# Queries of the first attention, pairs 2 to 7: seven half-size products for eight, with five weight sums read from DRAM

## The chip, the cores and the metric

The kernel runs on one core of a Trainium2 chip. The core has a matrix engine (TensorE, "PE" in the profile, with its weight loads as "PEld"), VectorE ("DVE"), ScalarE ("ACT"), GpSimd ("POOL") and SyncE ("SP"), whose queue does nothing here but start DMAs. Each engine works through its own instructions in order, and they wait for one another through semaphores. Matmuls write to PSUM, which has eight banks of 128 x 512 float32. [...]

The metric is the time of one execution in microseconds on the device. Before the change it is 1499.09 us (median of three runs, 1498.25 to 1500.35).

## The reference, cut to what matters

A token tensor `x` of 16 batches x 128 tokens x 512 passes through two layers, each an attention over a context of 16 x 128 x 128 and a feed-forward part with experts. All arithmetic is float32. What the change touches is the first attention:

```python
q_hk = (hidden_q @ Wq.T).reshape(b, s, H, K)            # H = 16 heads
q_big = jnp.einsum('bshk,hkq->bshq', q_hk, w_kc_q)
q_r = jnp.einsum('bshq,hqr->bhsr', q_big, W_qr)         # R = 64 per head
k_r = jnp.einsum('bld,hdr->bhlr', kv_rope, W_kr)
scores = jnp.einsum('bhsr,bhlr->bhsl', q_r, k_r)
attn = jax.nn.softmax(scores, axis=-1)
ctx_c = jnp.einsum('bhsl,bld->bhsd', attn, kv_rope)
ctx_lat = jnp.einsum('bhsd,hkd->bhsk', ctx_c, w_kc_kv)
out = ctx_lat.reshape(b, s, H * K) @ Wo.T
...
x = x + jnp.tanh(g_xattn[0]) * _L0_xattn_ref(_layernorm(x, axis=-1), ctx_512, ...)
```

## The kernel before, in words

The three weight matrices of the queries are multiplied together once, in the fold at the start: `fq` is a 512 x 1024 matrix (16 heads x 64), held as 128 partitions x 4 chunks x 1024. A query is then one product: 512 normalised features by 1024 columns.

Batches are taken in pairs `v` of two, 256 tokens. The queries of pairs 0 and 1 are made within the fold (`query` with 512 tokens). Those of pairs 2 to 7 are made in `keys_and_queries(v)`: for each of four banks, two head pairs by four chunks, eight matmuls with a 128x128 block of `fq` as weights and 256 tokens moving, then an eviction by VectorE or ScalarE in turn (`evacuate`), then two key matmuls into another bank and their eviction. A float32 matmul is two instructions in the profile (and two weight loads).

Pair 2's queries are made between the first softmaxes: `carry(0)`, two steps of `keys_and_queries(2)`, `score(2)`, `carry(1)`, the other two steps. From then on an outer loop goes over u = 1 to 8 with v = u - 1. One step, in program order:

- loads of two later x tiles; `gather` (context by weights) of the even batch of pair v, `score(2u)`, `turn(u + 1)` (transposes of the normalised tokens of a later pair into `xnT`), `combine_next`;
- the projections of pair v (`project`, itself seven products for eight) with the softmax of batch 2u between them (`soften` on ScalarE and GpSimd, `block` on VectorE), then `carry(2u)`;
- `combine_next`, `score(2u + 1)`, the remaining projections with that batch's softmax, then `carry(2u + 1)`;
- stores of pair v for later (`xk`), `combine_next`, at odd u the context for a later group (`load_kv`), and last `keys_and_queries(u + 1)`, for u = 2 to 6.

`carry(b)` sends 16 small DMAs (128-byte pieces) that finish the transposition of the softmax. `combine_next` prepares weights of the feed-forward part: it writes a prepared block to DRAM (`w1_kept`, `w2_kept`), loads another (`quarters`) and has GpSimd make its sums. All these DMAs go through `send`, on SP's queue.

The order on an engine is not left to the compiler in this stage: `matmul`, `transpose` and `send`, and VectorE work passed to `pin`, are held in program order from `score(0)` on. SP waits in that order for what a DMA needs, and everything behind it waits too. PSUM banks: four of tag `mm` (`mm_tile`), two `tr`, two `acc`. Scores use `mm`; queries of this loop `tr`, keys `acc`.

In the lines of the profile, L169 is every ordered matmul and L174 every ordered transpose (both helpers); L179 is `send`; L85 and L87 are the two branches of `evacuate`; L546 is a matmul of `fold_second`, L534 a transpose of the fold; L639 and L640 are GpSimd sums of `fold_outward`; L703 and L709 belong to `soften` and `block`.

Of the kernel before, what the change touches and what calls it, by code (L numbers as in the profile page):

```python
# [9 lines left out]
F32 = mybir.dt.float32  # L10
AF = mybir.ActivationFunctionType
ALU = mybir.AluOpType
# [3 lines left out]
P = 128  # L16
NB = 16
# [5 lines left out]
H = 16  # L23
# [19 lines left out]
def kernel(  # L43
# [22 lines left out]
    def tr_tile(name):  # L66
        return ps_tr.tile([P, 512], F32, tag="tr", name=name)
# [7 lines left out]
    def pin(ins):  # L75
        if pinned[0]:
            tc.keep_in_program_order(ins)
# [3 lines left out]
    def evacuate(dst, src):  # L81

        flip[0] ^= 1
        if flip[0]:
            pin(nc.vector.tensor_copy(dst, src))  # L85
        else:
            nc.scalar.copy(dst, src)  # L87
# [290 lines left out]
    with tc.tile_pool(name="a0", bufs=2) as ap, tc.tile_pool(name="a0s", bufs=3) as sp:  # L378
# [34 lines left out]
        def query(dst, p, xnT):  # L413
            for c in range(ND):
                matmul(
                    dst, fq[:, c, ts(p, P)], xnT[:, c, :],
                    start=(c == 0), stop=(c == ND - 1),
                )

        def homes(what, v):  # L420
            twos = [
                ap.tile([P, 2, 2 * P], F32, tag=f"{what}{j}", name=f"{what}_{v}_{j}", bufs=1)
                for j in range(NPAIR // 2)
            ]
            return [t[:, i, :] for t in twos for i in range(2)], twos
# [23 lines left out]
                xns[v].append(xn)  # L449

        def turn(v, which=(0, 1)):
            g, h = divmod(v, 2)
            if h == 0 and which[0] == 0:
                turned[g] = lnp.tile([P, ND, GT], F32, tag="xnT", name=f"xnT_a0_{g}", bufs=1)
            for i in which:
                xn = xns[v][i]
                tr = (acc_tile if v == 2 else tr_tile)(f"xtr_a0_{v}_{i}")
                for c in range(ND):
                    transpose(tr[:, ts(c, P)], xn[:, ts(c, P)], ident)
                dst = turned[g][:, :, ts(2 * h + i, P)]  # L460
                if v == 2:
                    pin(nc.vector.tensor_copy(dst, tr.rearrange("p (c t) -> p c t", t=P)))
                else:
                    evacuate(dst, tr.rearrange("p (c t) -> p c t", t=P))

# [199 lines left out]
        def score(b):  # L667


            v, i = divmod(b, 2)  # L670
            tiles = [mm_tile(f"s_ps{b}_{t}") for t in range(4)]
            for p in range(NPAIR):
                for j in range(2):
                    rows = slice(j * R, (j + 1) * R)
                    matmul(
                        tiles[p // 4 * 2 + j][:, ts(p % 4, P)],
                        q_r[v][p][rows, ts(i, P)], k_r[v][p][rows, ts(i, P)],
                        start=True, stop=True,
                    )
            ebs[b] = rp.tile([P, NK, H, BK], F32, tag="eb", name=f"eb_{b}")  # L680
            eTs[b] = rp.tile([P, NK, H, BK], F32, tag="eT", name=f"eT_{b}")
            soft[b] = []
            for t in range(4):
                nmx = sp.tile([P, 4], F32, tag="nmx", name=f"nmx_a0_{b}_{t}", bufs=4)
                pin(nc.vector.tensor_reduce(  # L685
                    nmx, tiles[t].rearrange("p (i l) -> p i l", l=P), AX.X, ALU.max,
                    negate=True,
                ))
                soft[b].append((tiles[t], nmx))
# [18 lines left out]
        def block(b, t):  # L708
            pin(nc.vector.transpose(  # L709
                ebs[b][:, :, 4 * t : 4 * t + 4, :].rearrange("p k n i -> p n k i"),  # L710
                soft[b][t].rearrange("p n (k i) -> p n k i", k=NK),
            ))
# [43 lines left out]
        def project(v, n):  # L756
# [17 lines left out]
            for i, cols in targets:  # L774
# [2 lines left out]
                    dst, y_ps, gate_x[0], dst, ALU.mult, ALU.add  # L777
                ))

        def keys_and_queries(v):  # L780
            g, h = divmod(v, 2)
            half = slice(2 * h * P, (2 * h + 2) * P)
            (k_r[v], k_two), (q_r[v], q_two) = homes("k", v), homes("q", v)
            for j in range(NPAIR // 2):
                q_ps = tr_tile(f"q_ps{v}_{j}")
                for i in range(2):
                    query(q_ps[:, ts(i, 2 * P)], 2 * j + i, turned[g][:, :, half])
                evacuate(q_two[j], q_ps.rearrange("p (i t) -> p i t", i=2))
                k_ps = acc_tile(f"k_ps{v}_{j}")
                for i in range(2):  # L790
                    key(k_ps[:, ts(i, 2 * P)], 2 * j + i, roped[g][1][:, half])
                evacuate(k_two[j], k_ps.rearrange("p (i t) -> p i t", i=2))
                yield j


# [61 lines left out]
        ups = {}  # L857

        xk = [wd.tile([P, D], F32, name=f"xk_{n}") for n in range(KEPT)]
        ordered[0] = pinned[0] = True  # L860


# [6 lines left out]
        for p in range(7):  # L869
            fold_next(p)  # L870

            if p in (3, 5):
                turn(2, (p // 2 - 1,))
            if p % 2 == 0:
                soften(0, p // 2)
                if p:
                    block(0, p // 2 - 1)
        score(1)
        fold_next(7)
        block(0, 3)  # L880
# [889 lines left out]
```

## Time and profile before

| | |
|---|---|
| median of three runs | 1499.09 us |
| profiled execution, its own time | 1500.14 us |
| its span in the profile | 1498.3 us |
| TensorE busy | 1477.4 us (99%), 6752 instructions |
| weight loads busy | 997.9 us (67%) |
| VectorE, ScalarE, GpSimd busy | 832.9, 436.9, 466.5 us |
| DMA moved | 163.50 MB, mean 109 GB/s |
| queries of pairs 2 to 7 (128x256) | 384 instructions, 86.9 us busy |

The profile is of one execution. In the rows of groups and of the timeline, `out<-in` are the program's tile names without numbers, then the shape, then a count. Matmuls are pipelined: the length of one is its way through the array, and the distance of two starts is what it costs when they follow one another. "PEclk" is the granted clock of TensorE, 9 for full in the slices and 1.00 in the windows. A row with "SPq" is the time in which SP issues the DMA, not that of the transfer.

### The profile page before, as it was taken

How to read it: one execution, taken by the hardware profiler on the slowest of the kernel's cores; microseconds unless marked ns; L12 is line 12 of the kernel's file. 1: busy time of each engine (PE TensorE's matmuls, PEld its weight loads, DVE VectorE, ACT ScalarE, POOL GpSimd, SP SyncE). 2: the span in 40 equal slices, each digit the busy share in tenths (PEclk: the TensorE clock that was granted, in tenths of full speed). 3: DMA queues.
4: the chain of work that ended last, by engine and by line, in shares of the span. 5: the costliest groups of instructions: out<-in, count | busy, mean ns of one | idle time of the engine just before them, and what ended most of it. 6: DMA issues, size and time to landing. Idle time of an engine off the chain costs nothing. (4 is left out here: it accounts for less than half of the span.)

```text
span 1498.3 us, 19508 instructions
## 1 busy us (share of the span) xinstructions
PE 1477.4 (99%) x6752; PEld 997.9 (67%) x6752; DVE 832.9 (56%) x1722; ACT 436.9 (29%) x1432; POOL 466.5 (31%) x500
## 2 busy tenths in 40 slices
PE   7999999999999999999999999999999999999999
PEld 5567778778877666876678666876668444444444
DVE  2274644654656555655564656455556776757422
ACT  1262432432441122012210321022203565545310
POOL 1153533623422233204320442124414333324200
PEclk9999999999999999999999999999999999999999
DMA  7533645344244822452246222721242342323212
GB/s 265 144 94 94 188 140 153 111 119 125 64 81 139 249 74 74 122 151 74 74 113 159 74 74 72 197 90 63 80 136 71 76 127 71 84 61 90 64 29 99
DMA packets 142274, 163.50 MB, mean 109 GB/s; under 512 B 54096, under 2 KB 102224, under 8 KB 140000
## 3 DMA queue, kind: packets, MB, share of 16 engines
q1 hardware_dynamic: 139024, 157.13, 36.5%
q0 software_dynamic: 2016, 4.13, 1.1%
q8 instruction: 54, 0.88, 0.3%
q10 hardware_dynamic: 1136, 0.99, 0.2%
q14 instruction: 44, 0.36, 0.1%
HBM read 106.35 MB, written 18.09 MB: 83 GB/s over the span
## 5 line engine op out<-in xcount | busy, mean ns | idle before, releaser
L1130 POOL TENSOR_TENSOR near<-base,a 128x512 f32<-128x512 f32 x32 | 42.6, 1332 | 345.0 <-ACT base L1127 233.5
L201 POOL TENSOR_TENSOR e<-e,rden_a 128x512 f32<-128x512 f32 x64 | 66.6, 1040 | 164.5 <-DVE rden_a L199 141.8
L169 PE MATMUL q_ps<-xnT_a,fq 128*128 128x256 f32 (+1 forms) x448 | 115.8, 410 | 0.0
L1127 ACT ACTIVATE a<-a 128x512 f32<-128x512 f32 x64 | 40.3, 630 | 256.8 <-DVE a L1126 256.8
L169 PE MATMUL l_ps<-t,b_sb 128*128 128x512 f32 x256 | 115.1, 592 | 0.0
L696 ACT ACTIVATE e<-s_ps,nmx_a 128x128 f32<-128x128 f32 x256 | 90.2, 386 | 78.0 <-DVE nmx_a L685 40.4
L194 ACT ACTIVATE e<-e,nmx_a 128x128 f32<-128x128 f32 x256 | 98.8, 387 | 34.7 <-DVE nmx_a L189 34.7
L1126 DVE TENSOR_TENSOR a<-l_ps,base 128x512 f32<-128x512 f32 x64 | 44.0, 688 | 108.0 <-PE l_ps L169 107.9
L169 PEld LDWEIGHTS q_ps<-xnT_a,fq 128*128 128x128 f32 x448 | 84.8, 190 | 24.5 <-issue 12.5
L703 POOL TENSOR_TENSOR e<-e,rden_a 128x512 f32<-128x512 f32 x64 | 66.0, 1039 | 100.7 <-DVE rden_a L701 100.7
L169 PEld LDWEIGHTS l_ps<-t,b_sb 128*128 128x128 f32 x256 | 48.6, 190 | 59.5 <-issue 57.6
L169 PE MATMUL fy_ps<-ring,far 128*128 128x256 f32 x384 | 87.2, 380 | 0.0
L169 PE MATMUL y_ps<-fo_raw,c 128*128 128x256 f32 x384 | 85.8, 380 | 0.9 <-DVE c L85 0.9
L776 DVE SCALAR_TENSOR_TENSOR x<-y_ps,gates,x 128x256 f32<-128x256 f32 x112 | 48.7, 477 | 67.0 <-PE y_ps L169 66.9
L1192 DVE SCALAR_TENSOR_TENSOR x<-fy_ps,gw,x 128x256 f32<-128x256 f32 x112 | 46.5, 475 | 69.3 <-PE fy_ps L169 69.3
L169 PEld LDWEIGHTS fy_ps<-ring,far 128*128 128x128 f32 x384 | 72.6, 190 | 13.6 <-issue 4.0
L169 PEld LDWEIGHTS y_ps<-fo_raw,c 128*128 128x128 f32 x384 | 72.3, 190 | 10.7 <-ACT c L87 1.0
L1344 DVE STREAM_TRANSPOSE eb<-e 128x512 f32<-128x512 f32 x64 | 45.5, 712 | 42.0 <-POOL e L201 37.4
L169 PE MATMUL ht_ps<-T,ring 128*128 128x256 f32 x256 | 65.7, 379 | 0.0
L169 PE MATMUL t_ps<-a,a_sb 128*128 128x512 f32 x128 | 65.4, 592 | 0.0
L169 PE MATMUL t_ps<-base,a_sb 128*128 128x512 f32 x128 | 65.4, 592 | 0.0
L169 PE MATMUL y_ps<-fo_sums,c 128*128 128x256 f32 x256 | 60.4, 385 | 2.1 <-ACT c L87 0.8
(257 smaller groups left out, 2956.3 us busy)
## 6 DMA issues: line engine op xcount, KB each, us to landing
ring<-w SPq DMA_DIRECT2D x32, 896.0 KB, 4.5
eT<-eb SPq DMA_DIRECT2D x312, 64.0 KB, 2.0
ring<-w SPq DMA_DIRECT2D x16, 1024.0 KB, 5.3
ring<-in_f_w SPq DMA_DIRECT2D x12, 1024.0 KB, 6.1
wq<-in_wq SPq DMA_DIRECT2D x8, 512.0 KB, 6.1
x<-in_x SPq DMA_DIRECT2D x16, 256.0 KB, 4.6
quarters<-in_f_w SPq DMA_DIRECT2D x32, 128.0 KB, 2.5
w<-sums SPq DMA_DIRECT2D x8, 512.0 KB, 3.6
```

Of the source, the lines that this page charges most:

```text
L169: ins = nc.tensor.matmul(*args, **kw)
L194: nc.scalar.activation(dst[:, ts(i, P)], src[:, ts(i, P)], AF.Exp, bias=nmx[:, i : i + 1], accum_out=den[:, i : i + 1],)
L201: nc.gpsimd.tensor_tensor(d3, d3, rden.unsqueeze(2).to_broadcast([P, 4, P]), ALU.mult)
L696: nc.scalar.activation(e[:, ts(i, P)], s_ps[:, ts(i, P)], AF.Exp, bias=nmx[:, i : i + 1], accum_out=den[:, i : i + 1],)
L703: nc.gpsimd.tensor_tensor(e3, e3, rden.unsqueeze(2).to_broadcast([P, 4, P]), ALU.mult)
L776: pin(nc.vector.scalar_tensor_tensor(dst, y_ps, gate_x[0], dst, ALU.mult, ALU.add))
L1126: nc.vector.tensor_tensor(a, l_ps, base, ALU.add)
L1127: nc.scalar.activation(a, a, AF.Gelu_apprx_tanh)
L1130: nc.gpsimd.tensor_tensor(mix, base, second, ALU.add)
L1192: nc.vector.scalar_tensor_tensor(dst, y_ps[:, ts(i, half)], q.first[:, t : t + 1], dst, ALU.mult, ALU.add,)
L1344: nc.vector.transpose(by_blocks(ebs[b])[:, :, 4 * j : 4 * j + 4, :].rearrange("p k n i -> p n k i"), e.rearrange("p (n k i) -> p n k i", n ...
```

## The change

The product of a pair, 256 tokens x 512 features x 1024 columns, is cut into halves in all three directions: features (two chunks each), columns (heads 0 to 7 and 8 to 15, `near_q` and `far_q`), tokens (the two batches). Of the eight products of halves, seven are made, from sums of halves, after Winograd's form of Strassen's method: each product is four column blocks by two chunks of matmuls with 128 tokens moving. The parts:

- `query_sums()`, before `score(0)`: four sums or differences of quarters of `fq` (each 128 x 1024), three on GpSimd and one on VectorE; five of the seven weights are written to DRAM in ten DMAs, four on SP's queue and six on GpSimd's. The near columns of `fq` stay in place as two weights; the far columns become two places of 512 KB for streamed weights.
- `fetch()`: two sends of 256 KB that bring the next streamed weight into the place just used. Two fetches are made before `score(1)`; after that one follows each product with a streamed weight. Over a pair the products are made in the order 4, 0, 5, 1, 3, 2, 6 and the streamed ones among them are 4, 5, 3, 2, 6.
- `query_product(v, n, ...)`: eight matmuls into one bank (`tr` for pair 2, `mm` for the others), the fetch, and the additions into the result: ScalarE copies for products 4, 0 and 3, VectorE additions from PSUM for products 0, 5, 1, 2 and 6, two GpSimd additions after product 3. `u_2` holds a partial sum, in the tag of the normalised tokens.
- `keys_and_queries`: two products ahead of the first and of the second group of keys, product 3 ahead of the third, product 2 ahead of the fourth, product 6 after it.
- `turn`: the transposed tokens are kept per pair instead of per group of four batches, and four sums of them are made beside, two on VectorE and two on GpSimd.

```diff
+            if what == "q":
+                whole = ap.tile([P, NPAIR, 2, P], F32, tag="q", name=f"q_{v}", bufs=1)
+                return [whole[:, p].rearrange("p i t -> p (i t)") for p in range(NPAIR)], whole
...
         def turn(v, which=(0, 1)):
-            g, h = divmod(v, 2)
-            if h == 0 and which[0] == 0:
-                turned[g] = lnp.tile([P, ND, GT], F32, tag="xnT", name=f"xnT_a0_{g}", bufs=1)
+            if which[0] == 0:
+                turned[v] = lnp.tile([P, 2, ND, 2 * P], F32, tag="xnT", name=f"xnT_a0_{v}", bufs=1)
...
-                dst = turned[g][:, :, ts(2 * h + i, P)]
+                dst = turned[v][:, 0, :, ts(i, P)]
...
+            if which[-1] == 1:
+                b11, b12, b21, b22 = [
+                    turned[v][:, 0, 2 * k : 2 * k + 2, ts(i, P)]
+                    for k in range(2) for i in range(2)
+                ]
+                t_1, t_2, t_3, t_4 = [
+                    turned[v][:, 1, n].rearrange("p (c t) -> p c t", t=P) for n in range(4)
+                ]
+                pin(nc.vector.tensor_tensor(t_1, b12, b11, ALU.subtract))
+                pin(nc.vector.tensor_tensor(t_2, b22, t_1, ALU.subtract))
+                nc.gpsimd.tensor_tensor(t_3, b22, b12, ALU.subtract)
+                nc.gpsimd.tensor_tensor(t_4, b21, t_2, ALU.subtract)
+                turned[v] = [b11, b21, t_4, t_1, t_2, t_3, b22]
...
+        streamed = (4, 5, 3, 2, 6)
+        fq_kept = {
+            (n, h): wd.tile([P, 2, 2 * P], F32, name=f"fq_{n}_{h}")
+            for n in streamed for h in range(2)
+        }
+        near_q, far_q = slice(0, H * R // 2), slice(H * R // 2, H * R)
+
+        def query_sums():
+            a11, a12 = fq[:, :2, near_q], fq[:, 2:, near_q]
+            a21, a22 = fq[:, :2, far_q], fq[:, 2:, far_q]
+            two = rp.tile([P, 2, 2, H * R // 2], F32, tag="eT", name="fq_sums")
+            s_1, s_2 = two[:, 0], two[:, 1]
+
+            def keep(n, src):
+                for h in range(2):
+                    begin = nc.sync if n in (2, 5) else nc.gpsimd
+                    begin.dma_start(out=fq_kept[n, h], in_=src[:, :, ts(h, 2 * P)])
+
+            keep(2, a22)
+            nc.gpsimd.tensor_tensor(s_1, a21, a22, ALU.add)
+            nc.vector.tensor_tensor(a21, a11, a21, ALU.subtract)
+            keep(5, a21)
+            nc.gpsimd.tensor_tensor(s_2, s_1, a11, ALU.subtract)
+            keep(3, s_1)
+            keep(4, s_2)
+            nc.gpsimd.tensor_tensor(a22, a12, s_2, ALU.subtract)
+            keep(6, a22)
+
+        fetched = []
+
+        def fetch():
+            n = len(fetched)
+            if n == 5 * (NB // 2 - 2):
+                return
+            rows = slice(n % 2 * 2, n % 2 * 2 + 2)
+            for h in range(2):
+                send(
+                    fq[:, rows, H * R // 2 + h * 2 * P : H * R // 2 + (h + 1) * 2 * P],
+                    fq_kept[streamed[n % 5], h],
+                )
+            fetched.append(fq[:, rows, far_q])
+
+        used = [0]
+
+        def query_product(v, n, q, u_2):
+            if n < 2:
+                w = fq[:, 2 * n : 2 * n + 2, near_q]
+            else:
+                w = fetched[used[0]]
+                used[0] += 1
+            ps = (tr_tile if v == 2 else mm_tile)(f"q_ps{v}_{n}")
+            for m in range(NPAIR // 2):
+                for c in range(2):
+                    matmul(
+                        ps[:, ts(m, P)], w[:, c, ts(m, P)], turned[v][n][:, c],
+                        start=c == 0, stop=c == 1,
+                    )
+            if n > 1:
+                fetch()
+            src = ps.rearrange("p (m t) -> p m t", t=P)
+            c11, c12, c21, c22 = [q[:, 4 * m : 4 * m + 4, i] for m in range(2) for i in range(2)]
+            if n == 4:
+                nc.scalar.copy(u_2, src)
+            elif n == 0:
+                pin(nc.vector.tensor_tensor(u_2, src, u_2, ALU.add))
+                nc.scalar.copy(c11, src)
+            elif n == 5:
+                pin(nc.vector.tensor_tensor(c21, src, u_2, ALU.add))
+            elif n == 1:
+                pin(nc.vector.tensor_tensor(c11, src, c11, ALU.add))
+            elif n == 3:
+                nc.scalar.copy(c22, src)
+                nc.gpsimd.tensor_tensor(c12, c22, u_2, ALU.add)
+                nc.gpsimd.tensor_tensor(c22, c22, c21, ALU.add)
+            else:
+                dst = c21 if n == 2 else c12
+                pin(nc.vector.tensor_tensor(dst, src, dst, ALU.add))
+
         def keys_and_queries(v):
...
-            for j in range(NPAIR // 2):
-                q_ps = tr_tile(f"q_ps{v}_{j}")
-                for i in range(2):
-                    query(q_ps[:, ts(i, 2 * P)], 2 * j + i, turned[g][:, :, half])
-                evacuate(q_two[j], q_ps.rearrange("p (i t) -> p i t", i=2))
+            u_2 = lnp.tile([P, NPAIR // 2, P], F32, tag="xn", name=f"u2_{v}")
+            for j, ns in enumerate(((4, 0), (5, 1), (3,), (2, 6))):
+                for n in ns[:2 if j < 2 else 1]:
+                    query_product(v, n, q, u_2)
                 k_ps = acc_tile(f"k_ps{v}_{j}")
...
+                if j == 3:
+                    query_product(v, 6, q, u_2)
                 yield j
...
+        query_sums()
         ordered[0] = pinned[0] = True
...
+        for _ in range(2):
+            fetch()
         score(1)
```

More of the change, by code (lines that the diff above doesn't have):

```diff
@@ L782, in keys_and_queries @@
             half = slice(2 * h * P, (2 * h + 2) * P)
-            (k_r[v], k_two), (q_r[v], q_two) = homes("k", v), homes("q", v)
-            for j in range(NPAIR // 2):
-                q_ps = tr_tile(f"q_ps{v}_{j}")
-                for i in range(2):
-                    query(q_ps[:, ts(i, 2 * P)], 2 * j + i, turned[g][:, :, half])
-                evacuate(q_two[j], q_ps.rearrange("p (i t) -> p i t", i=2))
+            (k_r[v], k_two), (q_r[v], q) = homes("k", v), homes("q", v)
+            u_2 = lnp.tile([P, NPAIR // 2, P], F32, tag="xn", name=f"u2_{v}")
+            for j, ns in enumerate(((4, 0), (5, 1), (3,), (2, 6))):
+                for n in ns[:2 if j < 2 else 1]:
+                    query_product(v, n, q, u_2)
                 k_ps = acc_tile(f"k_ps{v}_{j}")
```

## The prediction

> **What bounds the kernel now.** I read four views in this order: the page's first two parts, the timeline of TensorE around one pair's queries, the timeline of SP's queue over the same microseconds, and the list of DMA issues. The page says that TensorE is never free after the first slice:
>
> ```profile
> PE 1477.4 (99%) x6752; PEld 997.9 (67%) x6752; DVE 832.9 (56%) x1722; ACT 436.9 (29%) x1432; POOL 466.5 (31%) x500
> ...
> PE   7999999999999999999999999999999999999999
> ...
> PEclk9999999999999999999999999999999999999999
> ```
>
> So a matmul that goes saves its time, and a wait that comes is paid in full. The timeline of TensorE (start, length, instruction, count) shows pair 3's queries and keys, made at the end of outer step u=2:
>
> ```profile
> 188.20 3.62 PE L169 MATMUL q_ps<-xnT_a,fq 128*128 128x256 f32 x16
> 191.65 1.03 PE L169 MATMUL k_ps<-kvT,wkr_sb 128*128 128x256 f32 x4
> ...
> 205.46 3.60 PE L169 MATMUL c_ps<-eT,kvr 128*128 128x512 f32 x8
> ```
>
> By starts, 16 query instructions take 191.65 - 188.20 = 3.45 us (216 ns each), four key instructions 0.86 us, and the pair 205.46 - 188.20 = 17.26 us without a gap. SP's queue in the same stretch:
>
> ```profile
> 191.97 11.20 SPq L179 DMA_DIRECT2D eT<-eb  x16
> 203.21 1.08 SPq L179 DMA_DIRECT2D xk<-x  x2
> 204.34 0.44 SPq L179 DMA_DIRECT2D w<-quarters  x1
> 204.87 0.40 SPq L179 DMA_DIRECT2D w<-sums  x1
> 207.21 1.96 SPq L179 DMA_DIRECT2D quarters<-in_f_w  x4
> 209.22 0.95 SPq L179 DMA_DIRECT2D x<-in_x  x2
> ```
>
> The reader should see that SP is taken for all the time in which TensorE makes the queries: 16 small transfers of `carry(odd)` cost it about 0.63 us each to issue, then come the kept rows and `combine_next`. Today nobody waits for that. The order is the program's (`send` pins it).
>
> **The products.** Now a pair costs 4 x 16 instructions of 256 columns, 13.8 us by the 3.45 us above. The change makes it 7 products of 4 x 2 matmuls of 128 columns, two instructions each: 112. Whether halving the columns halves the time is seen where `fold_second` does just that, 128 columns with new 128x128 weights every time:
>
> ```profile
> 42.67 2.05 PE L546 MATMUL f_ps<-m,wq 128*128 128x128 f32 x16
> 44.56 0.27 PE L534 MATMUL mtr<-ident,mT 128*128 128x128 f32 x1
> ```
>
> From the first start to the one after the 16th is 1.89 us, the first interval a long one; the last 15 starts stand 111 ns apart. So a product is 16 x 0.111 = 1.78 us, seven are 12.5 us, 1.35 us less per pair and 8.1 us in six pairs. Bounds: 0.107 (half of 216: 1.8 us a pair) and 0.190, one weight load's length if loads did not overlap (7.5 us a pair lost). I take 0.111, the same shape.
>
> **The stream.** Five of seven weights come from DRAM through two places. Weights 4 and 5 were fetched in the pair before; weight 3 may be fetched once product 4 is done, 2 after 5, 6 after 3. These sends stand in `keys_and_queries`, so on SP they come after `carry(odd)`, the kept rows and `combine_next`: at u=2 not before 209.2. A fetch is two sends of 256 KB; the DMA view (KB each, us to landing):
>
> ```profile
> eT<-eb SPq DMA_DIRECT2D x312, 64.0 KB, 2.0
> ...
> quarters<-in_f_w SPq DMA_DIRECT2D x16, 256.0 KB, 3.3
> ...
> x<-xk SPq DMA_DIRECT2D x8, 256.0 KB, 4.8
> ```
>
> With 0.45 us until the second send begins and 3.3 to 4.8 to land, weights are there 3.8 to 5.3 us after SP is free, with a share of a busy queue up to 5.5; I take 4.5. TensorE meets product 3 after products 4, 0, 5, 1 and two key groups: 4 x 1.78 + 2 x 0.86 = 8.85 us after the pair's start. Start of the queries, SP free, and wait before product 3 (free + 4.5 - start - 8.85), for u = 2 to 6:
> 188.20, 209.2: 16.6 us; 243.19, 260.0: 12.4; 297.31, 315.4: 13.7; 351.76, 367.6: 11.5; 405.77, 421.1: 11.0. Together 65.2 us. SP's times are the ends of the last row of `combine_next` (u=3: of the `kv` load, 259.54 + 0.42). The wait does not shrink by itself: `carry(odd)` starts 1.4 to 3.8 us after the queries do, because its last `block` stands behind the last projection's evictions on VectorE, so it moves with TensorE.
>
> Behind the waiting matmul stand keys, products 2 and 6, then the next step's `gather` and `score`: all of TensorE. On SP the fetch of 6 waits for product 3, and behind it stand the next pair's 4 and 5 and the next x loads, which have most of a step to spare.
>
> **After the wait.** Left are products 3, 2, 6 and two key groups, 3 x 1.78 + 2 x 0.86 = 7.07 us. Weight 6 is asked for when product 3 ends and needs 4.5 us; TensorE has 0.86 + 1.78 + 0.86 = 3.5 us of work meanwhile, so at full clock 1.0 us is waited and the pair ends 8.1 us after weight 3 lands. The clock is the second price. The start of the run, stretch by stretch (length, busy time of PE, PEld, DVE, ACT, POOL, clock, DMA):
>
> ```profile
> 16.00:20.00 4.00, 2.02 (x14) 1.27 (x15) 2.34 (x7) 1.84 (x3) 0.00 (x0) 0.68 1.05 385
> 20.00:24.00 4.00, 4.00 (x17) 3.25 (x16) 0.97 (x2) 0.96 (x2) 0.00 (x0) 0.50 0.61 213
> 24.00:28.00 4.00, 4.00 (x32) 3.29 (x31) 2.04 (x4) 1.23 (x3) 0.00 (x0) 0.97 0.03 8
> ```
>
> With TensorE half idle up to 20 the granted clock fell to 0.50 and stayed there through 24, with TensorE fully busy again. A gap of 11 us should do the same. Between no loss and 3.4 us (the whole half-clock stretch, 0.32 x 4 / 0.5 + 4 = 6.6 us, spent working) I take 5.1 us at half clock after a gap, 2.55 us lost. The wait for weight 6 then vanishes (product 3 takes 3.56, weight 6 lands at about 7.8, where TensorE arrives), and the pair ends 9.6 us after weight 3. So a pair ends at SP free + 4.5 + 9.6 against the old 205.46, 260.46, 314.58, 369.02, 423.03: later by 17.8, 13.6, 14.9, 12.7 and 12.2, together 71.2 us. The 1.35 us per pair is already in it: everything before product 3 is hidden by the wait.
>
> [...]
>
> **Pair 2** is interleaved with the first softmaxes, its sends with `carry(0)` (SP from 98.78 to 109.2) and `carry(1)` (109.3 to 119.3). With everything 2 us late (next part), queries start at 98.0, and TensorE is through 4, 0, 5, 1, two key groups and `score(2)` (2.0) at 108.9. The fetch of 3 leaves after `carry(0)`, at 111.2, and lands at 115.7: 6.8 us waited. The fetch of 6 comes behind `carry(1)`, which starts at 113.2 and ends at 123.4: landing at 127.9, another gap of 4 to 6 us. Product 6, with some 0.8 us lost to the clock, ends at 130.5 against the old 115.48: +15, the 2 included. `carry(2)` starts later by the same and still is long done when `gather(2)` needs it.
>
> **Sums of weights, at the start.** POOL: three adds of 128x1024 at 2.4 us (the `s<-c,c` row, 2398 ns) and six issues at 0.5 (`eT<-eb` on POOL's queue, 498 ns): 10.2 us from the last `fq` copy at 72.9 to 83.1. POOL's first fold sum ran at 81.37 after 38.3 us idle, so it slips 1.7 us, and the `soften`/`block` chain with it. VectorE: one 128x1024 subtraction, 1.4 us (1404 ns), after the last query of group 0 at 76.8, ahead of the maxima that started at 77.90. I take 2 us; 0 if the slack takes both, 6 if POOL begins only after that query.
>
> **Edits that I cost at nothing.** The token sums per pair (two VectorE of 128x256 at 0.42, two POOL at 0.73) and the evictions (3 ScalarE copies at 0.58, 5 VectorE adds at 0.69, 2 POOL adds at 1.33, in place of 2 and 2 copies) lie in a stretch in which TensorE waits or has 17 us of work; uncovered they would be at most 0.5 us a pair, 3 in all. The VectorE add of product 2 must wait for POOL's two adds, done 3.2 us after product 3, before `score` (it has `gather`'s 3.5 us in front). The 15 MB more of transfers fit: the DMA share is 2 to 4 tenths here.
>
> **Sum:** 71.2 + 15 = 86 us on the profiled execution's 1500.1 (span 1498.3 and 1.8 around it); that execution is 1.0 above the median 1499.1, so 1585.
>
> **Rivals.** A, the other side: the weights arrive in time. That needs SP free 4.3 us after the queries start (8.85 - 4.5); the rows show 15.3 to 21.0. If it were so: 1499 - 8.1 + 2 = 1493. It would need the sends to overtake the queue, and the pinned order speaks against it. B: loads of weights do not overlap in this stream, 0.190 instead of 0.111: hidden before product 3, but 16 x 0.079 x 3 = 3.8 us a pair after it, +23: 1608. The 15 even starts of `fold_second` speak against it. C: the waits are as said, but the clock holds and the sums hide: 8.1 instead of 9.6 (5 x 1.5), 4 less in pair 2, 2 less at the start, -13.5, and -3 if weights land in 4.0: 1568.
>
> **How the numbers follow.** Main case 0.73, C 0.16, B 0.08, A 0.03. On the main case, the upper bounds add 1.0 us of landing (7 times), 0.9 of clock (5 times), 4 at the start and 3 of uncovered edits: 1603; the lower is C's 1568, with a few us for places where TensorE's small gaps of today (0.5 to 0.9 us a step) vanish in the wait. Range 1560 to 1606. About 0.2% (3 us) is what a measurement tells from no change: faster 0.03 (A), same 0.01 (A with its gain eaten), slower 0.96.
>
> **What would show it.** In TensorE's timeline a gap of 11 to 17 us in pairs 3 to 7 before the fifth product, ended by a DMA into `fq`; PEclk below 9 in those slices; on SP, `fq` rows directly after `quarters`/`w` rows; products at 1.78 us. I am wrong if the `fq` rows stand ahead of `eT<-eb`, or if TensorE waits for something else first, such as VectorE's adds or a PSUM bank.

## The result, and the profile after

The changed kernel takes 1584.37 us (median of four runs, 1583.3 to 1584.78) against 1499.38 for the kernel before: a ratio of 1.0566, 95% interval 1.0548 to 1.0584. The forecast was 1585.

The page of the kernel after, its first two parts, its costliest group and its row of the new DMAs:

```profile
PE 1487.6 (94%) x7040; PEld 1014.3 (64%) x7040; DVE 854.2 (54%) x1753; ACT 440.5 (28%) x1438; POOL 501.1 (32%) x533
...
PE   7988969696797999999999999999999999999999
...
PEclk9988979898998999999999999999999999999999
...
L169 PE MATMUL q_ps<-xnT_a,fq 128*128 128x128 f32 (+1 forms) x736 | 123.0, 329 | 72.2 <-DMA fq<-fq 69.8
...
fq<-fq SPq DMA_DIRECT2D x64, 256.0 KB, 3.6
```

TensorE, which was busy all the time, now has a hole in about every other slice of the first third, and the clock falls in nearly all of these slices. The group row says who ends the holes: 69.8 us of waiting for `fq<-fq`, the streamed weights. The span grew by 83.2 us (1498.3 to 1581.5), so these waits are most of it.

TensorE's timeline around pair 3's queries, the place shown of before (the brackets hold the wait and what ended it):

```profile
207.10 3.73 PE L169 MATMUL q_ps<-xnT_a,fq 128*128 128x128 f32 x32
...
231.41 3.75 PE L169 MATMUL q_ps<-xnT_a,fq 128*128 128x128 f32 x16 [15.27 <-DMA fq<-fq]
234.95 1.91 PE L169 MATMUL k_ps<-kvT,wkr_sb 128*128 128x256 f32 x4
236.66 2.10 PE L169 MATMUL q_ps<-xnT_a,fq 128*128 128x128 f32 x16
...
241.25 3.60 PE L169 MATMUL c_ps<-eT,kvr 128*128 128x512 f32 x8
```

and SP's queue beside it:

```profile
211.52 10.02 SPq L179 DMA_DIRECT2D eT<-eb  x16
...
225.59 1.97 SPq L179 DMA_DIRECT2D quarters<-in_f_w  x4
227.66 14.30 SPq L179 DMA_DIRECT2D fq<-fq  x10
242.01 1.06 SPq L179 DMA_DIRECT2D x<-in_x  x2
```

Product 3 stands 15.27 us until its weight has landed, and SP begins to send that weight at 227.66, after the 16 sends of `carry(odd)`, the kept rows and `combine_next`. The pair takes 34.15 us where it took 17.26. Product 3's own 3.75 us for 16 instructions is the half clock, which the windows show (columns: stretch, length, busy time of the five engines, clock, DMA share, GB/s):

```profile
216.00:220.00 4.00, 0.14 (x1) 0.00 (x0) 0.07 (x1) 0.59 (x1) 0.00 (x0) 0.99 0.47 106
220.00:224.00 4.00, 0.00 (x0) 0.00 (x0) 0.00 (x0) 0.00 (x0) 0.00 (x0) 0.50 0.63 192
...
232.00:236.00 4.00, 4.00 (x18) 3.82 (x18) 0.00 (x0) 0.59 (x1) 0.14 (x1) 0.50 0.39 127
236.00:240.00 4.00, 4.00 (x28) 3.72 (x27) 1.38 (x2) 0.34 (x1) 2.39 (x2) 0.88 0.34 96
```

The five pairs of the loop, from the timelines (the last column is the pair's length beyond the 17.26, 17.27, 17.27, 17.26 and 17.26 us of before):

| u | queries start | first send of weight 3 | product 3 starts | its wait | end of pair | longer by |
|---|---|---|---|---|---|---|
| 2 | 207.10 | 227.66 | 231.41 | 15.27 | 241.25 | 16.9 |
| 3 | 278.62 | 296.73 | 301.75 | 14.10 | 310.57 | 14.7 |
| 4 | 347.63 | 365.60 | 369.18 | 12.52 | 378.41 | 13.5 |
| 5 | 415.59 | 430.17 | 434.91 | 10.29 | 443.71 | 10.9 |
| 6 | 480.46 | 494.72 | 498.03 | 8.54 | 507.69 | 10.0 |

These are 66 us. Pair 2, counted from the last group of fold queries to `gather(0)`, takes 60.10 us (72.09 to 132.19) for 42.30 (73.18 to 115.48): 17.8 more. Its fetches wait on SP behind `carry(0)` and `carry(1)`; products 3 and 6, which start at 115.84 and 128.65, follow the two `fq` rows:

```profile
101.34 10.99 SPq L179 DMA_DIRECT2D eT<-eb  x16
112.44 2.58 SPq L179 DMA_DIRECT2D fq<-fq  x4
115.11 10.25 SPq L179 DMA_DIRECT2D eT<-eb  x16
125.46 7.49 SPq L179 DMA_DIRECT2D fq<-fq  x6
```

The stretch up to pair 3 is 2.2 us longer, and the fold's end lies 1.1 us earlier in this profile. Together 84.9 us; at the `gather` behind pair 7 the two timelines stand 84.66 us apart (507.69 and 423.03).

### The profile page after: what moved, and what is told of

Its sections match the earlier page's. It is cut to its first block, busy times and chain, and to the rows that moved or that the text cites. A ratio compares the mean times of both kernels' runs of the same rounds, so it can differ in the third digit from the quotient of the medians.

```text
span 1581.5 us, 20302 instructions
## 1 busy us (share of the span) xinstructions
PE 1487.6 (94%) x7040; PEld 1014.3 (64%) x7040; DVE 854.2 (54%) x1753; ACT 440.5 (28%) x1438; POOL 501.1 (32%) x533
## 5 line engine op out<-in xcount | busy, mean ns | idle before, releaser
L169 PE MATMUL q_ps<-xnT_a,fq 128*128 128x128 f32 (+1 forms) x736 | 123.0, 329 | 72.2 <-DMA fq<-fq 69.8
L169 PEld LDWEIGHTS q_ps<-xnT_a,fq 128*128 128x128 f32 x736 | 104.5, 216 | 90.7 <-issue 87.2
L718 POOL TENSOR_TENSOR e<-e,rden_a 128x512 f32<-128x512 f32 x64 | 66.2, 1044 | 73.3 <-DVE rden_a L716 73.3
L791 DVE SCALAR_TENSOR_TENSOR x<-y_ps,gates,x 128x256 f32<-128x256 f32 x112 | 48.5, 475 | 61.6 <-PE y_ps L169 61.5
```

The source lines that it names most:

```text
L169: ins = nc.tensor.matmul(*args, **kw)
L718: nc.gpsimd.tensor_tensor(e3, e3, rden.unsqueeze(2).to_broadcast([P, 4, P]), ALU.mult)
L791: pin(nc.vector.scalar_tensor_tensor(dst, y_ps, gate_x[0], dst, ALU.mult, ALU.add))
```

## The experiments

The theory: TensorE waits because the fetches stand last on SP's queue, and what follows a wait runs at half clock; the products themselves are cheaper than the old ones. The rivals: the transfers are slow wherever they are sent; the clock is the larger price; something else of the change (its sums, its evictions, its banks) costs time that the waits now hide. All medians of the kernel before beside these runs lie between 1498.39 and 1499.06.

### The fetches on ScalarE's queue

```diff
             for h in range(2):
-                send(
-                    fq[:, rows, H * R // 2 + h * 2 * P : H * R // 2 + (h + 1) * 2 * P],
-                    fq_kept[streamed[n % 5], h],
-                )
+                tc.keep_in_program_order(nc.scalar.dma_start(
+                    out=fq[:, rows, H * R // 2 + h * 2 * P : H * R // 2 + (h + 1) * 2 * P],
+                    in_=fq_kept[streamed[n % 5], h],
+                ))
```

> The streamed weights are fetched from ScalarE's queue instead of SP's; nothing else differs from the changed kernel. Queue theory (the fetches were late because they stood on SP behind carry(odd), xk and combine_next): the wait before product 3 goes in all six pairs, about 1 us per pair remains for weight 6, so before minus 8.1 for the products, plus 6 for weight 6, plus 2 to 4 for the start: 1500, between 1495 and 1508. Transfer theory (two places and 512 KB per weight are too slow whoever issues them, or they lose to the other transfers): the waits stay at 8 us or more per pair, 1560 to 1585.

Measured: 1524.49 us, ratio 1.0171 (1.0156 to 1.0186). The waits went as the theory says, from 69.8 to 4.1 us, the longest 1.1; so the transfers are fast enough and the place on the queue was the cause of the waits. But the time is above what was expected, because new waits came. The list of TensorE's waits between 55 and 520 us (total, times, longest):

```profile
PE c_ps L169 <- DVE x L791: 9.2, 3, 3.5
PE y_ps L169 <- DVE c L85: 4.7, 3, 3.5
PE q_ps L169 <- DMA fq<-fq: 4.1, 6, 1.1
```

`gather` waits for a bank that VectorE empties late, and the half clock follows: after the waits of 3.50 and 2.25 us the next two instructions take 2.08 us both times (1.12 in the run without a stream, at 227.39), and the 16 behind them 4.34 and 4.43 for 3.62. GpSimd's timeline of the same run shows what VectorE stands behind:

```profile
224.96 0.72 POOL L920 TENSOR_TENSOR sums<-quarters 128x256 f32<-128x256 f32 x1 [3.87 <-DMA w<-sums]
...
227.69 0.72 POOL L920 TENSOR_TENSOR sums<-quarters,sums 128x256 f32<-128x256 f32 x1
228.37 2.04 POOL L718 TENSOR_TENSOR e<-e,rden_a 128x512 f32<-128x512 f32 x2
```

The feed-forward sums of `combine_next` wait for a store, and the softmax multiplication (L718) stands behind them on GpSimd; `block`, which needs it, stands ahead of the projections' evictions on VectorE. In the kernel before the order is the same, but the sums are done in time: the multiplication starts at 219.30, 13.8 us after `gather` does (205.46); here it is 17.8 (228.37 and 210.55). Whether this order costs the time is tested next.

### The same, with GpSimd's sums behind the softmax multiplication

This run also holds GpSimd's multiplications and feed-forward sums in program order (`pin`); the lines below show the moved sums only.

```diff
-        def combine_next():
+        def combine_next(owed=None):
...
-                sum_quarters(t - 1, *quarters[t - 1])
+                if owed is None:
+                    sum_quarters(t - 1, *quarters[t - 1])
+                else:
+                    owed.append(t - 1)
...
             soft_step(now, 2)
+            for t in owed:
+                sum_quarters(t, *quarters[t])
```

> The fetch on ScalarE's queue as in the first experiment, and GpSimd's feed-forward sums of a step moved behind the softmax multiplication of its score blocks. Theory (the first experiment's loss of some 22 us came from GpSimd's sums, late for their load, standing ahead of that multiplication): the waits of c_ps on project's evictions go, the half clock at the ends of the steps goes with them, and the time is 1499 to 1507 us. Rival (the loss is that of ten sends on ScalarE's queue ahead of its copies): 1518 us or more. In between, both had a part.

Measured: 1504.71 us, 1.0038 (1.0025 to 1.0051), 20 us less than the run before. GpSimd's timeline, the same place:

```profile
222.28 2.04 POOL L718 TENSOR_TENSOR e<-e,rden_a 128x512 f32<-128x512 f32 x2
224.59 1.04 POOL L718 TENSOR_TENSOR e<-e,rden_a 128x512 f32<-128x512 f32 x1 [0.28 <-DVE rden_a L716]
225.59 0.73 POOL L920 TENSOR_TENSOR sums<-quarters 128x256 f32<-128x256 f32 x1
```

The multiplication now starts 12.4 us after `gather` (209.85), the second set of sums comes after it, and the waits of `c_ps` on L791 are gone. So the loss on ScalarE's queue was one of order on GpSimd: with TensorE no longer held up, the sums wait for stores that SP sends late (`w<-sums` 0.7 and 9.7 us after `gather` starts in the first experiment, 0.6 us ahead of it and 6.1 after in the kernel before), and the softmax stands behind them.

### Sends of carry, kept rows and combine_next behind the fetch of weight 6

At u = 3 the context load goes behind all products too, in this run, the next, and those built on them.

```diff
-            if u < last:
-                carry(odd)
-            if v < KEPT // 2:
...
+            def behind():
+                if u < last:
+                    carry(odd)
+                if v < KEPT // 2:
...
                 for p in keys_and_queries(u + 1):
+                    if p == 2:
+                        behind()
```

> Fetches stay on SP, but in pairs 3 to 7 carry(odd), the xk stores and the last combine_next of a step stand behind the fetch of weight 6, and the context load behind all products; pair 2 is as in the changed kernel. Queue theory: the 66 us that pairs 3 to 7 gained over before go, and 0.3 more per pair for the products: 1584.4 - 67 = 1517, between 1510 and 1525; carry(odd) ends some 23 us after the start of the queries, and gather of the odd batch comes 30 us after it, so it does not wait. Rival (the delay only moves: carry(odd) becomes late for gather, or SP does not catch up in the next step): a wait for eT of 5 us or more per step, 1540 or above.

Measured: 1510.27 us, 1.0074 (1.0057 to 1.0091), some 7 us below the middle of what was expected and at its lower end. In TensorE's timeline the pair is whole (start, length), and takes 219.97 - 204.01 = 15.96 us, 1.30 less than before the change:

```profile
204.01 3.73 PE L169 MATMUL q_ps<-xnT_a,fq 128*128 128x128 f32 x32
...
212.88 1.95 PE L169 MATMUL q_ps<-xnT_a,fq 128*128 128x128 f32 x16
...
219.97 3.60 PE L169 MATMUL c_ps<-eT,kvr 128*128 128x512 f32 x8
```

and on SP the fetches lead:

```profile
205.09 10.28 SPq L179 DMA_DIRECT2D fq<-fq  x6
215.47 11.28 SPq L179 DMA_DIRECT2D eT<-eb  x16
```

`carry(odd)` still has time enough behind them. 74 of the 85 us were a matter of which send stands first. What is left is pair 2, whose fetches still stand behind `carry(0)` and `carry(1)`: 8.9 us of waiting for `fq`.

### Only the kept rows and combine_next behind the fetch

```diff
+            def behind():
+                if v < KEPT // 2:
+                    for n in (2 * v, 2 * v + 1):
+                        send(xk[n], xs[n])
+                for _ in range(0 if u >= last - 1 else 1 if u > 1 else 2):
+                    combine_next()
+
             if u < last:
                 carry(odd)
```

> Only xk, the last combine_next and the context load go behind the fetch of weight 6; carry(odd) stays ahead of the fetches. Queue theory, by the rows of the changed kernel between the end of carry(odd) and the first fetch (6.1, 5.4, 4.1, 3.1, 2.2 us for pairs 3 to 7): 21 us less, 1563, between 1557 and 1568. Rival (carry's 16 transfers of 128-byte pieces hold up the DMA engines, not SP): hardly any gain, above 1575.

Measured: 1564.0 us, 1.0439 (1.0422 to 1.0456). Pairs 3 to 7 wait 8.76, 6.41, 8.08, 5.83 and 6.31 us before product 3, 35.4 in place of 60.7. So of the 74 us, 20 belong to the sends of `combine_next`, the kept rows and the context load, and 54 to `carry(odd)`, taken in this order.

### No stream

```diff
-            for h in range(2):
+            for h in range(2 if n < 2 else 0):
```

> All fetches after the first two are left out, so products 3, 2 and 6 and those of later pairs take whatever weights lie in the two places (the scores are then of other weights); every product, sum, addition and eviction is as in the changed kernel. If the stream is the whole loss: before - 8.1 + 2 to 4 for the start = 1494, between 1490 and 1499. If additions, banks or the half-size matmuls cost something beside it: above 1502.

Measured: 1501.89 us, 1.0017 (1.0008 to 1.0027): about 8 us more than the middle of what was expected and outside its range, and no faster than the kernel before. The stream costs 82.5 us of the changed kernel; the rest of the change, which was to gain 6, loses 2.8. The timelines of this run say where: the five pairs of the loop gain 1.3 us each, 6.5; pair 2 loses 5.9, and the stretch between pairs 3 and 4 is 3.25 us longer, with waits behind GpSimd's late sums (the softmax multiplication starts 15.4 us after `gather`), the effect that the second experiment isolates. In pair 2 are the start sums (1.56 us), a wait of 2.4 us for a bank (below), its half clock (1.6), 1.4 for VectorE's last additions, less the 1.3.

The bank: in pair 2 the second product (weight 0) waits for a bank that `fold_next(7)`, the last output fold, holds until VectorE has read it. The same wait stands in the kernel after:

```profile
100.84 3.46 PE L169 MATMUL q_ps<-xnT_a,fq 128*128 128x128 f32 x16 [2.40 <-DVE fo_sums L653]
```

### The wait filled with matmuls

```diff
             ps = (tr_tile if v == 2 else mm_tile)(f"q_ps{v}_{n}")
+            if n == 3 and v > 2:
+                for _ in range((62, 58, 51, 41, 33)[v - 3]):
+                    matmul(ps[:, :P], fq[:, 0, :P], turned[v][0][:, 0], start=True, stop=True)
```

> The changed kernel with idle work on TensorE in the gap before product 3 of pairs 3 to 7: 62, 58, 51, 41, 33 matmuls of 128 columns with weights that lie there, into the bank that product 3 overwrites, so that some 1.2 us of each gap stay and the clock has no reason to fall. Clock theory: what the five pairs lose after weight 3 has landed is the half clock (2.8, 1.7, 2.2, 1.7, 2.6 us by the clock's own records, 11 together), and about 1 us per pair of waiting for weight 6 comes in its place: 1584.4 - 6 = 1578, between 1574 and 1581, with PEclk at full after u=2. Rival (the slow end of a pair comes from additions or from weight 6, the clock costs nothing): 1583 to 1587.

Measured: 1578.92 us, 1.0529 (1.0513 to 1.0545). The same stretch as above in its windows:

```profile
224.00:228.00 4.00, 4.00 (x38) 4.00 (x37) 0.00 (x0) 0.00 (x0) 0.52 (x1) 1.00 0.88 324
228.00:232.00 4.00, 1.96 (x18) 1.77 (x16) 0.00 (x0) 0.00 (x0) 2.29 (x4) 1.00 0.87 244
232.00:236.00 4.00, 3.99 (x19) 3.81 (x20) 0.00 (x0) 0.58 (x1) 0.14 (x1) 0.59 0.61 174
```

The clock holds through the filled part, and the kernel is 5.5 us faster for 490 more instructions that do nothing: the clock is a real part of the price, but a small one. The filling was a little short: 2.04 us of idle were left here and 1.48 in pair 5, each followed by some 3.5 us at half clock (by the starts, the products and keys behind them take 1.76 us longer in both places). So 5.5 is rather a lower figure for what the clock costs in five pairs.

### The sends behind the fetch, and pair 2's fetches on ScalarE's queue

The order of the third experiment, and for the five fetches that pair 2 triggers:

```diff
+                if 2 <= n < 7:
+                    tc.keep_in_program_order(
+                        nc.scalar.dma_start(out=dst, in_=fq_kept[streamed[n % 5], h])
+                    )
+                else:
+                    send(dst, fq_kept[streamed[n % 5], h])
```

> As e2_carry_behind, and the fetches made within pair 2 (weights 3, 2, 6 and the next 4, 5) go to ScalarE's queue, so that carry(0) to carry(2) have SP for themselves. Queue theory: pair 2 ends as it did in e1_act_queue, 45.9 us after the last query group of the fold began instead of 59.5: 1510.3 - 13.6 = 1497, between 1493 and 1501. Rival (with TensorE never waiting, the feed-forward sums on GpSimd, which stand behind the two additions of product 3 and ahead of the softmax's multiplication, hold up block and the projections as in e1_act_queue): 1500 to 1512.

Measured: 1499.57 us, 1.0002 (0.9993 to 1.001). No wait for `fq` is left, and the kernel stands where the kernel before stood. The bank wait of 2.4 us remains, but in this profile no half clock follows it: the product behind it, at 101.94, takes 1.86 us to the next group.

### The last output fold ahead of the fetches

```diff
+        fold_next(7)
         for _ in range(2):
             fetch()
         score(1)
-        fold_next(7)
         block(0, 3)
```

> As e6_mix, and fold_next(7) is made ahead of score(1), so that the banks that product 0 of pair 2 needs are evicted ahead of the maxima on VectorE. If the 2.4 us wait and the 1.7 us of half clock at product 0 come from that order: 4 us less than e6_mix, 1493, between 1489 and 1498. If the place is set by the sums of weights on GpSimd at the start instead: as e6_mix or above, since the softmax of batch 1 starts later.

Measured: 1496.68 us, 0.9986 (0.9977 to 0.9995). The bank wait is gone (0.8 us is left, on GpSimd's sum) and the mean clock of the profile is 1.0, and the kernel is 2.9 us faster than the run before, where about 4 were expected; 3.7 us are missing to the 1493 expected. From the last fold queries to `gather(0)` it takes 45.75 us, 3.45 more than before the change.

### Without GpSimd's sums at the start

```diff
-            nc.gpsimd.tensor_tensor(s_1, a21, a22, ALU.add)
...
-            nc.gpsimd.tensor_tensor(s_2, s_1, a11, ALU.subtract)
-            keep(3, s_1)
-            keep(4, s_2)
-            nc.gpsimd.tensor_tensor(a22, a12, s_2, ALU.subtract)
+            keep(3, a12)
+            keep(4, a11)
```

> This is the version with the fold first, with GpSimd's three sums of whole tiles at the start left out; the ten stores to DRAM are kept, but two of them store single weights where sums stood, so the queries of pairs 3 to 7 use wrong weights. Theory (GpSimd's sums at the start delay the first folds): the last fold's q_ps group starts about 1.1 to 1.6 us earlier than in the version with the fold first, VectorE's xn_a operation there is back at about 0.55 us each, and the time is 1495 us (1494 to 1496). Rival (the start is delayed by the ten stores' issues or by VectorE's sum): no change, 1496.7 us (1496 to 1497.5).

Measured: 1493.2 us, 0.9967 (0.9954 to 0.9979), and 42.54 us from the last fold queries to `gather(0)`: 3.2 less, which is nearly all that was missing. (The profiled execution itself took 1495.8 us; behind `gather(0)` it is 3.0 us longer than the one with the sums.) VectorE's `xn_a` operation, as a group (ns of one: least, median, most; when), first with the sums, then without:

```profile
L448 DVE TENSOR_SCALAR xn_a<-x,mv_a,rstd_a x2: 864/1716/2569, 74.6 to 75.4; 128x512 f32<-128x512 f32 x2
```

```profile
L448 DVE TENSOR_SCALAR xn_a<-x,mv_a,rstd_a x2: 544/546/547, 73.1 to 73.5; 128x512 f32<-128x512 f32 x2
```

The expectation took an earlier start of the last fold queries for a sign of this. They do start 1.51 us earlier, but so does TensorE's group at 40.22 (41.73 with the sums), before any sum, so that shift has another cause and says nothing on the sums. What the sums cost lies behind the fold: VectorE's operation, with the maxima and the first evictions of the output fold behind it, and GpSimd's own first fold sum, 11.4 us after the last fold queries against 8.2.

### The sums cut by fold, in the same buffer

```diff
-            nc.gpsimd.tensor_tensor(s_1, a21, a22, ALU.add)
+            for j in range(4):
+                m = ts(j, P)
+                for dst, a, b, what in (
+                    (s_1, a21, a22, ALU.add), (s_2, s_1, a11, ALU.subtract),
+                    (a22, a12, s_2, ALU.subtract),
+                ):
+                    nc.gpsimd.tensor_tensor(dst[:, :, m], a[:, :, m], b[:, :, m], what)
...
```

> The version with the fold first, with GpSimd's three sums of 128x1024 at the start cut into twelve of 128x256, each issued when the fold that completes its columns is copied, so that nine of them can run while TensorE still folds. Theory (VectorE's xn_a operation waits there for the end of a GpSimd sum, and GpSimd comes late to the sums of the output fold): xn_a at most 0.55 + 0.75 us, GpSimd's first fold sum within 9 us of the last fold's q_ps group where it took 11.4, 2 to 3 us less than the version with the fold first, as when those sums were left out: 1494 us (1492.5 to 1495.5). Rival (the ten stores or VectorE's sum set it): 1496.7 us (1496 to 1498).

Measured: 1499.6 us, 1.0004 (0.9994 to 1.0013): a miss, and slower than uncut. No sum ran beside the fold. GpSimd's first one, VectorE's sum behind them, and TensorE behind that:

```profile
72.14 1.41 POOL L820 TENSOR_TENSOR fq_sums<-fq 128x256 f32<-128x256 f32 x2 [29.15 <-PE f_ps L561]
```

```profile
80.33 2.41 DVE L824 TENSOR_TENSOR fq<-fq 128x1024 f32<-128x1024 f32 x1 [3.93 <-POOL fq_sums L820]
```

```profile
83.12 6.71 PE L169 MATMUL o_ps<-wo,wckv_all 128*128 128x512 f32 x8 [2.92 <-DVE cb_kq L85]
```

The first row names the reason: the sums wait for TensorE's last matmul of the fold. Their result has the tag `eT`, and that pool lies over the buffers of the fold's weights, which TensorE reads until 72 us. So the place of a result, not its inputs, set the time.

### The sums cut by fold, in a buffer that is free

```diff
-            two = rp.tile([P, 2, 2, H * R // 2], F32, tag="eT", name="fq_sums")
-            s_1, s_2 = two[:, 0], two[:, 1]
+            s_1, s_2 = [
+                fo_sums[:, n, 4:].rearrange("p (c h) d -> p c (h d)", c=2) for n in range(2)
+            ]
...
```

> As the version with the sums cut by fold, with their two results in a part of fo_sums that is free until the output fold, and not in a buffer that lies over the query fold's last weights (there all sums waited for TensorE's last reading of these, and VectorE's sum for them). Theory: nine of twelve sums run at some 0.7 us each between 44 and 72 us, GpSimd is free before the output fold's first sums (first one within 9 us of the last fold's q_ps group), VectorE's xn_a operations there take under 1.3 us each, and the time is 1494 us (1492.5 to 1495.5). Rival (what was saved by leaving the sums out was something else): 1496 us or more.

Measured: 1494.16 us (1492.66 to 1495.82), 0.997 (0.9958 to 0.9981): the fastest version that computes the whole reference, faster than both kernels. GpSimd's timeline shows sums between the folds and the first one of the output fold (L654) at 80.73, 9.6 us after the last fold queries at 71.12:

```profile
50.34 0.72 POOL L821 TENSOR_TENSOR fo_sums<-fq 128x256 f32<-128x256 f32 x1 [9.36 <-ACT fq L565]
...
70.91 0.72 POOL L821 TENSOR_TENSOR fo_sums<-fq 128x256 f32<-128x256 f32 x1 [4.66 <-ACT fq L565]
...
78.42 1.40 POOL L821 TENSOR_TENSOR fq<-fq,fo_sums 128x256 f32<-128x256 f32 x2 [4.08 <-DMA fq<-fq]
80.12 0.68 POOL L812 DMA_DIRECT2D fq<-fq  x1 [0.30 <-DVE fo_raw L647]
80.73 0.83 POOL L654 TENSOR_TENSOR fo_sums<-fo_raw,fo_sums 128x256 f32<-128x256 f32 x1
```

It was expected within 9 us: two of the last sums still wait for a store of the quarter that they overwrite. The two `xn_a` operations together take 1.45 us where they took 3.35. From the last fold queries to `gather(0)` it is now 43.74 us, 1.4 more than before the change, which with the 6.5 us gained in the five pairs gives 5.1; measured are 4.3.

## Why the prediction was right, by its steps

- **Products.** 1.78 us each was right: 32 instructions start within 3.58 us, 112 ns apart, and where nothing waits a pair is 1.30 us shorter (1.35 was said). Rival B, weight loads that do not overlap, falls with that.
- **The stream.** The wait before product 3 was to be 65.2 us in five pairs and is 60.7. Its terms: SP free after the queries start, 85.5 us in all for 87.1, the differences being -0.4, +1.3, -0.1, -1.3 and -1.1 (at u = 2 and 3 `carry`'s 16 sends took 10.0 and 11.2 us for 11.2 and 10.0, at u = 5 and 6 the four `w<-sums` 2.0 for 2.9 and 2.7); landing of weight 3 after its first send, 4.08 us in the mean for 4.5; and 9.03 us of TensorE's work before it for 8.85. The third and fourth experiments show that the queue's order is the cause, and how it divides.
- **After the wait.** 9.27 us in the mean for 9.6. No wait for weight 6, as said, and half clock that costs 2.8, 1.75, 2.2, 1.7 and 2.6 us, 11.0 together, for 12.75. Rival C, a clock that holds, falls; with the clock held by filling, the kernel is still at 1578.9. It stayed half for 3.4 to 5.6 us after TensorE resumed; the 2.55 us a pair, an estimate chosen between no loss and 3.4, was on the high side of the mean loss of 2.2.
- **Pair 2.** +15 was said, +17.8 is measured. The wait before product 3 is 4.26 us for 6.8, the one before product 6 is 4.82 for 4 to 6. SP's rows of pair 2 account for the 2.8 us between: counted from the last fold queries, `carry(0)` starts 3.65 us later than before where the sum had 2; its sends and the fetch behind them take 0.7 us longer each, `carry(1)` 0.15, and product 6 lost 1.8 us to the clock for 0.8; against that, weight 6 landed in 3.2 us for 4.5. `carry(0)` starts when VectorE's last transposition of batch 0 ends. That is late by some 1.9 us from the start sums and, by VectorE's rows, by the token sums of `turn` ahead of it (0.79 us at 92.74 and 1.15 at 93.56), which I had costed at nothing. The sum also had no wait of 2.4 us for a bank at 100.84, nor the half clock behind it; I had not gone through who holds the two `tr` banks that pair 2 uses. In this kernel they lengthen nothing by the rows, since without them product 3 would only wait longer for SP; they cost where the fetches do not stand behind `carry`.
- **Behind pair 2.** 2.2 us more, of which `gather` at half clock is 1.2 (4.78 for 3.60); the sum ended the loss at the pair.
- **The start.** 2 us was said and 1.56 is there, but the argument had another mechanism. I set GpSimd's sums against GpSimd's own next work; the larger part by the rows is that VectorE's two `xn_a` operations take 3.35 us beside them for 1.09 without. Leaving them out is worth 3.2 us where nothing else hides it, above the 2 and within the 0 to 6. In the last experiment, where VectorE's part is gone and a wait of 0.8 us for GpSimd's sums stays, 2.0 of the 3.2 us went; the two were not tried apart. GpSimd's first fold sum slipped by 3.2 us (from 8.2 to 11.4 after the last fold queries) for the 1.7 said.
- **Edits at nothing.** In pairs 3 to 7 of the changed kernel they cost nothing that shows, since the waits hide them; in pair 2 the token sums cost, as said. The price named for lost cover, 3 us in all, left out the queue on GpSimd: without the waits its late feed-forward sums go with a loss of 3.25 us in one step of the run without a stream, and with 20 us in the run on ScalarE's queue. GpSimd's two additions after product 3 (1.3 us each) are not what makes them late: in the latter run they end at 209.49, and the sums start at 217.26, behind a store. The transfers added are 18.4 MB and not 15, since that figure left out the stores of the five weights.
- **Rival A.** Weights in time were priced at 1493. With the weights in time by sends alone, the versions stand at 1524.5 and 1499.6; with GpSimd's order mended the first is at 1504.7, with the output fold moved the second at 1496.7, and only with the start sums out of the way too at 1494.2. So that price was right for a kernel with two more edits, and 7 to 31 us too low for one that only gets its weights in time.

That 1585 and 1584.4 lie so close is partly luck: 5.2 us too much in the five pairs stand against 2.8 too little in pair 2 and 2.2 behind it, and the run's start and its stretch after pair 7 are 2.6 us shorter in this profile.

## What to carry to other kernels

A streamed operand is priced by the place of its send on the queue that issues it: list what stands ahead of it, with the issue time of each, and compare that with when the engine arrives, before looking at the transfer's own time. Here moving sends that nobody waited for behind the one that TensorE waits for was worth 74 of 85 us. When a wait goes away, what it hid comes into the open (a bank held by an earlier stage, an engine's sums ahead of the softmax, a buffer that lies over one still read), so the gain of a cheaper product arrives only when each of these has been moved as well.

## What the runs showed of the hardware

- VectorE's `tensor_scalar` of 128x512 took 0.864 and 2.569 us beside GpSimd's sums of 128x1024, 0.546 without them. GpSimd's two sums end at 75.17 and 77.67 us there, and VectorE's two operations at about 75.5 and 77.95: each ends just after the GpSimd sum in whose time it began. Beside sums of 128x256 the two take 1.81 us together where these run on (tenth experiment), and 1.45 in the last. So an operation that takes 0.546 us alone ends some 0.3 us after the sum; what holds it up was not shown.
- The clock fell after short waits too: after the 2.4 us wait at 100.84 in pair 2 (0.57 between 100 and 104), after 2.04 us in the filled run (0.59 between 232 and 236), and there after 1.48 and another 0.49 us in pair 5 (the eight instructions ahead of the second wait take 1.16 us, the eight behind it 1.80). Gaps of 2.74 and 1.14 us in the same run were not followed by it (16 instructions in 2.05 us each time, where the 15.27 us wait left 3.75), nor was the bank wait of 2.4 us in the run with pair 2's fetches on ScalarE's queue (1.86 us from product 0, at 101.94, to the next group). What decides between these was not tried.
- 16 sends of 64 KB take SP 10.0 to 11.3 us, 0.63 to 0.70 each, though one lands in 2.0 us.
